# A two-step graph layer: the first step's guess kept as a logarithm, and the packed list's flags made by one comparison

## The chip, the cores and the metric

The kernel runs on one NeuronCore of a Trainium2 chip. A core has five engines that work on their own queues, each in order, [...]: TensorE (PE in the profile; its weight loads are PEld), VectorE (DVE), ScalarE (ACT), GpSimd (POOL) and SyncE (SP, which here only starts DMAs). The metric is the time of one execution on the device in microseconds (us); three runs of the kernel before gave 1349.75, 1350.31 and 1355.44 us, median 1350.31 us.

## The reference, cut to what matters

The input is x (3327 rows of 256) and a sparse matrix adj (3327 x 3327, about four entries in a row beside the diagonal). The rows are normalised and rectified, and a graph layer of two steps runs on the result h:

```python
R = S + eye(N);  R = R / R.sum(-1)            # S is adj
for n in range(2):
    A = top_p_attention(Xa, W1, W2, W3)       # softmax of q k^T, only the largest entries
    Xf = R @ Xf                               # that make up 0.9 of a row's sum
    Xa = A @ Xa
    Z = Z + Xf @ U1[n].T + Xa @ U2[n].T
out = x + layernorm(h + Z) * ln_g + ln_b
```

In each row of the attention the entries are kept from the largest down until their sum reaches 0.9 of the whole. So each row needs a threshold: the value below which the entries sum to at most 0.1 of the row's total Z.

## The kernel before, in words

The 3327 rows are padded to 26 tiles of 128 rows (NP = 3328 columns). For each of the two steps and each tile the kernel makes the 128 x 3328 exponentials `e` of the logits, finds each row's threshold, sets what is below it to zero, turns `e` on TensorE (`Sums.turn`, L809, copied out of PSUM by ScalarE at L811) and multiplies it with the node features (`Sums.sum`, L823).

**The threshold.** It is not searched for by sorting. `guessed` (L616) makes a first guess for each row from Z and from moments of the logits (the columns `ms` that `project` makes on GpSimd at L541 to L545). All the working values are columns of one small tile `g` of 128 x 17, named `col(k)`. In step one, `measured_once` (L635) then sends two passes over the row through ScalarE (L633, once Relu, once Sign) to measure how much lies under the guess, and moves the guess with what they gave; the result is `col(16)`. `settle` (L723) uses it: VectorE keeps what is under the guess in `w` (L729), takes the eight largest of each of 20 segments (L734), the 40 largest of those (L741, L743), finds the exact threshold among them, and masks `e` in place (L763). `prove` checks at the end of each step that every row's threshold is certain; a flag that counts the failing rows decides at the very end whether a second program (`search_graph_layer`) does the whole layer anew by bisection. In step two `measured_twice` takes three passes; the change does not touch it.

**The sparse product.** adj is not multiplied as a whole. `listed` (L836) finds, for each of the 26 rows of tiles, which columns hold an entry: VectorE takes the largest absolute value of each column strip (L853) and `max` gives a list of up to 16 columns per partition. Four of them are fetched directly; those from the fifth on (`DIRECT` to `LIST`) are packed together over the partitions. For that, `over[:, t]` counts how many a partition has beyond four (L865), `packed` (L870) has TensorE sum these counts over the partitions in front (matmul with `upto`, L875; ScalarE copies the sum at L876), and VectorE makes a 128 x 128 matrix `oh` of flags: flag (p, k) is set where place k lies among the places that partition p fills, that is between the sum and the sum plus the count (two comparisons, L879 and L880). `gathered` (L882) uses `oh` in a matmul, picks one column number per partition and writes it as the fifth index (L893, L894). Then GpSimd starts gathers (indirect DMAs): five of columns of adj (`ac`, L900) and five of rows of the features (`xg`, L921) for each tile in step one, and five of `xg` in step two. `diffuse` (L929) multiplies them.

**What sets the order.** The order is written out by hand. Each piece of work is a Python generator, and each `yield` ends one portion of it. `PLAN[step]` holds seven strings (slots k = 0 to 6) for a tile; each letter takes one portion: `m` measured, `d` settle, `c` settle's remainder of the tile before, `w` the exponentials, `q` the next tile's queries, `p` packed, `h` gathered, `a` listed, `g` one gather, `e` first_end, `s` spread, `o` asked_for. In step one:

```python
PLAN = (("gmdsssa", "gmcdsssa", "edawwpg", "gmsdga", "gmspdea", "ohgdawwqg", "gehmgq"), ...
```

So `measured_once` of the tile after the current one takes its portions in slots 0 (guess), 1 (Relu pass), 3 (Sign pass), 4 and 6, and `packed` in slots 2 and 4; ten gathers are spread over the seven slots. Every engine executes its instructions in the order of this text (a dependency between neighbours is added at L1236). Each gather also waits for the last ScalarE instruction that the text has ahead of it (L1209), so that the gathers are spaced out. The tiles `ac` and `xg` have two buffers each, the transposed `eT` three, the PSUM tile `pt` two.

Of the kernel before, what the change touches and what calls it, by code (L numbers as in the profile page):

```python
# [9 lines left out]
F32 = mybir.dt.float32  # L10
# [3 lines left out]
AF = mybir.ActivationFunctionType  # L14
ALU = mybir.AluOpType
# [3 lines left out]
P = 128  # L19
# [4 lines left out]
NP = NT * P  # L24
# [6 lines left out]

SCALE = 1.9
BITS = 27
FIRST = 2.0 ** -7
assert 0.1 * SCALE / N > 2.0 ** -15


# [1 line left out]
def search_graph_layer(  # L39
# [13 lines left out]
    nc = tc.nc  # L53
# [8 lines left out]
    small = ctx.enter_context(tc.tile_pool(name="small", bufs=4))  # L62
# [85 lines left out]
    def nucleus(es, z):  # L148
        n = len(es)
        thr = small.tile([P, 2], F32, tag="thr", name="thr")  # L150
        cand = small.tile([P, 2], F32, tag="cand", name="cand")
        ncand = small.tile([P, 2], F32, tag="ncand", name="ncand")
        over = small.tile([P, 2], F32, tag="over", name="over")
        cnt = small.tile([P, 2], F32, tag="cnt", name="cnt")
        mass = small.tile([P, 2], F32, tag="mass", name="mass")
        low = small.tile([P, 2], I32, tag="low", name="low")
        candi = cand.bitcast(I32)
        nc.vector.tensor_scalar(thr, z, TOP_P, None, ALU.mult)
        nc.vector.memset(cand, FIRST)
        for k in range(BITS - 1, -1, -1):  # L160

            nc.vector.tensor_scalar(ncand, cand, -1.0, None, ALU.mult)
            for a in range(n):
                ja = scan.tile([P, NP], U8, tag="ja", name="ja")
                nc.scalar.activation(ja, es[a], AF.Relu, bias=ncand[:, a : a + 1],
                                     accum_out=over[:, a : a + 1])
                jv = scan.tile([P, NP], U8, tag="jv", name="jv")
                nc.vector.tensor_scalar(jv, es[a], cand[:, a : a + 1], None, ALU.is_ge, ALU.add,
                                        accum_out=cnt[:, a : a + 1])
            nc.vector.tensor_tensor(mass, cand, cnt, ALU.mult)  # L170
            nc.vector.tensor_tensor(mass, mass, over, ALU.add)
            nc.vector.tensor_tensor(low, mass, thr, ALU.is_lt)

            nc.vector.tensor_scalar(low, low, k, (1 << k) >> 1,
                                    ALU.logical_shift_left, ALU.bitwise_or)
            nc.vector.tensor_tensor(candi, candi, low, ALU.bitwise_xor)

        rc = small.tile([P, 2], F32, tag="rc", name="rc")  # L180
        nc.vector.reciprocal(rc, cand)
        nc.vector.tensor_scalar(ncand, cand, -1.0, None, ALU.mult)
        lim = small.tile([P, 2], F32, tag="lim", name="lim")
        for a in range(n):
            c = slice(a, a + 1)
            e = es[a]
            nc.vector.scalar_tensor_tensor(e, e, cand[:, c], e, ALU.is_ge, ALU.mult,
                                           accum_out=mass[:, c])
            eq = scan.tile([P, NP], U8, tag="jv", name="eq")
            nc.vector.tensor_scalar(eq, e, cand[:, c], None, ALU.is_equal)  # L190
            nth = scan.tile([P, NP], I16, tag="nth", name="nth")
            nc.vector.tensor_tensor_scan(nth, eq, eq, 0.0, ALU.add, ALU.max)

            nc.vector.tensor_sub(lim[:, c], thr[:, c], mass[:, c])
            nc.vector.scalar_tensor_tensor(lim[:, c], lim[:, c], rc[:, c], nth[:, NP - 1 : NP],
                                           ALU.mult, ALU.add)
            nc.vector.tensor_scalar(lim[:, c], lim[:, c], 1.0, None, ALU.add)
            nc.vector.scalar_tensor_tensor(eq, nth, lim[:, c], eq, ALU.is_ge, ALU.mult)
            nc.vector.scalar_tensor_tensor(e, eq, ncand[:, c], e, ALU.mult, ALU.add)
# [113 lines left out]
BIG = 1.0e30  # L313
LNBIG = 69.0
# [2 lines left out]
ROUNDS = (5, 6)  # L317
PG = (0.72168716, 3.51308980, -3.48705157)
PK = (3.57528079, -2.54929187, 0.86603878)
OFFSET = (18.0, 14.0)  # L320
TOPK = 8 * max(ROUNDS)
LNY = 0.25 * math.log(0.72)

# [6 lines left out]
FIRST = 8 * P  # L330
# [6 lines left out]
DIRECT = 4  # L337
LIST = 16
# [7 lines left out]
def guess_graph_layer(ctx, tc, x, adj, w1t, w2t, w3t, u1t, u2t, ln_g, ln_b, out, flag):  # L346
    nc = tc.nc
# [14 lines left out]
    V, G, S, PE = nc.vector, nc.gpsimd, nc.scalar, nc.tensor  # L362
# [265 lines left out]
    def con(k):  # L628
        return one[:, k : k + 1]
# [5 lines left out]
    def measured_once(r):  # L635
        e, ms = r["e"], r["ms"]


        col = guessed(r, small.tile([P, 17], F32, tag="g", name="g"))
        S.activation(col(4), col(2), AF.Square, bias=con(4))  # L640
        S.activation(col(11), col(4), AF.Identity, scale=ms(5), bias=ms(6))
        S.activation(col(1), col(0), AF.Exp, scale=-1.0, bias=con(5))
        G.tensor_scalar(col(7), col(9), 0.5, None, ALU.mult)
        G.tensor_scalar(col(8), col(9), 0.5 * NP, None, ALU.mult)
        G.tensor_scalar(col(5), col(1), OFFSET[0], None, ALU.mult)
        G.tensor_scalar(col(10), col(9), col(5), 1.0, ALU.mult, ALU.add)
        yield
        oa = small.tile([P, 3], F32, tag="oa", name="oa")
        through(e, AF.Relu, col(9), -1.0, oa[:, 0:1])
        yield  # L650
        through(e, AF.Sign, col(9), -1.0, oa[:, 1:2])
        yield
        S.activation(col(3), oa[:, 0:1], AF.Identity, scale=-1.0, bias=col(8))
        S.activation(col(4), oa[:, 1:2], AF.Relu, scale=col(7), bias=col(3))
        S.activation(col(6), col(4), AF.Ln, scale=col(1), bias=con(2))
        S.activation(col(3), col(4), AF.Square, scale=col(1), bias=con(1))
        S.activation(col(3), col(3), AF.Ln, scale=0.5, bias=col(10))
        S.activation(col(3), col(3), AF.Identity, scale=-1.0, bias=col(6))
        S.activation(col(3), col(3), AF.Exp, scale=col(11))
        yield  # L660

        V.tensor_scalar(col(5), oa[:, 1:2], NP - 31.0, BIG, ALU.is_gt, ALU.mult)
        V.tensor_scalar(col(6), col(4), col(1), 0.35, ALU.mult, ALU.is_lt)
        V.scalar_tensor_tensor(col(5), col(6), BIG, col(5), ALU.mult, ALU.add)
        V.tensor_scalar(col(3), col(3), 1.0e20, col(9), ALU.min, ALU.mult)
        V.tensor_tensor(col(16), col(3), col(5), ALU.add)

    def measured_twice(r):
        e, ms = r["e"], r["ms"]
# [166 lines left out]
    def listed():  # L836
# [10 lines left out]
        for k, (t, j0, n) in enumerate(pieces):  # L847
            at = ahead
            if k + 1 < len(pieces):
                ahead = asked(*pieces[k + 1])  # L850
            if j0 == 0:
                fm = small.tile([P, NT], F32, tag="fm", name="fm", bufs=2)
            V.tensor_reduce(fm[:, j0 : j0 + n], at[:, :n], AX.X, ALU.max, apply_absolute_value=True)  # L853
            if j0 + n < NT:
                yield
                continue
            V.scalar_tensor_tensor(fm, fm, 0.0, back, ALU.is_gt, ALU.mult)
            V.memset(fm[:, t : t + 1], 0.0)
            ls = lists[:, t, :]
            V.max(ls[:, :8], fm)  # L860
            V.match_replace(fm, ls[:, :8], fm, 0.0)
            V.max(ls[:, 8:LIST], fm)
            G.tensor_scalar(index[:, t, :DIRECT], ls[:, :DIRECT], -1.0, float(NONE), ALU.mult, ALU.add)
            of = small.tile([P, LIST], F32, tag="of", name="of", bufs=2)
            V.tensor_scalar(of[:, DIRECT:], ls[:, DIRECT:LIST], 0.0, None, ALU.is_gt, ALU.add,  # L865
                            accum_out=over[:, t : t + 1])
            done.append(t)
            yield

    def packed(t):  # L870

        assert t in done
        ls, ov = lists[:, t, :], over[:, t : t + 1]
        pb = ps_t.tile([P, 4, P], F32, tag="pt", name="pb")
        PE.matmul(pb[:, 0, :1], upto, ov, start=True, stop=True)  # L875
        S.copy(ls[:, LIST:], pb[:, 0, :1])  # L876
        yield
        ohs[t] = oh = small.tile([P, P], F32, tag="oh", name="oh", bufs=2)
        V.tensor_scalar(oh, place, ov, ls[:, LIST:], ALU.subtract, ALU.is_lt)  # L879
        V.scalar_tensor_tensor(oh, place, ls[:, LIST:], oh, ALU.is_ge, ALU.mult)  # L880

    def gathered(t):  # L882
        oh = ohs.pop(t)
# [7 lines left out]
        yield  # L891
        of = small.tile([P, LIST], F32, tag="of", name="of", bufs=2)
        V.scalar_tensor_tensor(of[:, :n], place[:, :n], nth, lo, ALU.is_equal, ALU.mult, accum_out=nth)  # L893
        G.tensor_scalar(index[:, t, DIRECT:], nth, -1.0, float(NONE), ALU.mult, ALU.add)  # L894

    def adjacent(t):
# [83 lines left out]
        V.tensor_copy(flag, pf[:1, 0, :1])  # L980

    own_of = {}
    live, ohs, acs, xgs, done, early = {}, {}, {}, {}, [], {}
    none = iter(())

    def run(work, n=99):
# [294 lines left out]
```

## Time and profile before

| | us |
|---|---|
| median of three runs | 1350.31 |
| the profiled execution | 1350.64 |
| its span, first to last instruction | 1348.9 |
| TensorE matmul busy | 1268.1 |
| VectorE busy | 1186.8 |
| ScalarE busy | 1081.0 |
| GpSimd busy | 997.2 |
| mean granted TensorE clock | 0.982 |

Step one's tiles run from about 100 to 745 us, the turn to step two until about 850 us, step two's tiles to the end. A busy time is the time in which an engine had an instruction in work. Matmuls are pipelined and their ends are modelled, so their busy times overlap, and spans on GpSimd are rough. A row of the timeline gives the start in us, the length in us, the engine, the line, the operation and its operands, and in brackets how long the engine had been idle and what ended the wait ("issue": nothing that the profile shows).

### The profile page before, as it was taken

What the parts mean: (1) busy time and instruction counts of PE and PEld (TensorE: products, weight loads), DVE (VectorE), ACT (ScalarE), POOL (GpSimd) and SP (SyncE); (2) the same over time, 40 slices, a digit from 0 to 9 for tenths busy, and PEclk for the clock granted to TensorE, in tenths of its full rate; (3) what the DMA queues carried; (4) which work ended last, traced back from release to release, by engine and by line L of the source; (5) the groups of instructions that cost most, each with busy time, mean ns of one, the idle gap of its engine ahead of it and who ended that gap; (6) DMA issues with size and microseconds to landing.
All of it is one profiled execution on the core that took longest, in us unless ns stands there. A gap on an engine that the chain in (4) does not pass through costs nothing.

```text
span 1348.9 us, 22270 instructions
## 1 busy us (share of the span) xinstructions
PE 1268.1 (94%) x6495; PEld 976.0 (72%) x6495; DVE 1186.8 (88%) x3637; ACT 1081.0 (80%) x2368; POOL 997.2 (74%) x1399
## 2 busy tenths in 40 slices
PE   5989899999999999999999579999999999999985
PEld 4635687877778777787877457777777777777774
DVE  6877899999999999999990689899998999999993
ACT  5475788798888879888863789899998999999841
POOL 5114788888878878887873578888888888888832
PEclk9999999999999999999999779999999999999998
DMA  8644545455454544445332212221212222122200
GB/s 277 221 157 141 160 136 144 134 144 147 133 153 133 140 138 142 144 135 152 106 104 86 75 55 60 78 89 54 91 59 85 62 82 90 52 91 64 81 21 24
DMA packets 92645, 149.79 MB, mean 111 GB/s; under 512 B 15425, under 2 KB 59072, under 8 KB 92512
## 3 DMA queue, kind: packets, MB, share of 16 engines
q1 hardware_dynamic: 75056, 105.37, 24.6%
q0 software_dynamic: 16640, 42.69, 12.1%
q8 instruction: 54, 0.88, 0.3%
q14 instruction: 79, 0.65, 0.2%
q10 hardware_dynamic: 816, 0.20, 0.1%
HBM read 120.93 MB, written 27.28 MB: 110 GB/s over the span
## 4 chain that ended last, share of the span: by engine, by line
PE 51%; DVE 20%; ACT 12%; POOL 11%; issue 3%; DMA 2%; SPq 0%; POOLq 0%; DVEq 0%; ACTq 0%
PE pa L823 22%; ACT ja L633 7%; PE pl L600 7%; PE pt L809 6%; PE pr L929 5%; POOL xg L921 5%; DVE w L729 4%; PE pz L942 3%; DVE cand L734 3%; DVE e L763 3%; PE pz L1011 2%; POOL g L676 2%; DVE bb L741 1%; DVE cand L743 1%; ACT e L604 1%
## 5 line engine op out<-in xcount | busy, mean ns | idle before, releaser
L823 PE MATMUL pa<-xw,eT 128*128 128x256 f32 x1352 | 323.6, 384 | 3.6 <-DVE s L953 3.6
L633 ACT ACTIVATE ja<-e,g 128x3328 uint8<-128x3328 f32 x106 | 325.7, 3072 | 0.1
L823 PE MATMUL pa<-x,eT 128*128 128x256 f32 x1352 | 323.1, 380 | 0.0
L823 PEld LDWEIGHTS pa<-xw,eT 128*128 128x128 f32 x1352 | 250.7, 190 | 52.5 <-issue 14.4
L823 PEld LDWEIGHTS pa<-x,eT 128*128 128x128 f32 x1352 | 243.7, 191 | 25.8
L734 DVE MAX8 cand<-w 128x8 f32<-128x168 f32 (+1 forms) x1040 | 253.7, 319 | 0.0
L811 ACT COPY eT<-pt 128x512 f32<-128x512 f32 (+1 forms) x364 | 199.5, 555 | 48.8 <-PE pt L809 47.7
L921 POOL DMA_INDIRECT xg<-bx,index x130 | 188.7, 1451 | 54.7 <-issue 24.4
L900 POOL DMA_INDIRECT ac<-in_adj,index x130 | 162.9, 1253 | 63.8 <-issue 28.2
L809 PE MATMUL pt<-ident,e 128*128 128x128 f32 x1144 | 176.6, 277 | 17.3 <-DVE e L760 9.4
L809 PEld LDWEIGHTS pt<-ident,e 128*128 128x128 f32 x1144 | 139.8, 144 | 60.5 <-issue 36.0
L921 POOL DMA_INDIRECT xg<-vx,index x130 | 152.5, 1173 | 34.3 <-issue 30.3
L729 DVE SCALAR_TENSOR_TENSOR w<-e,g 128x3328 f32<-128x3328 f32 x44 | 162.7, 3698 | 3.1 <-ACT g L714 3.0
L929 PE MATMUL pr<-xg,ac 128*128 128x257 f32 (+1 forms) x520 | 141.0, 395 | 8.4 <-DVE s L1119 6.8
L763 DVE SCALAR_TENSOR_TENSOR e<-e,rec 128x3328 f32<-128x3328 f32 x40 | 148.3, 3707 | 0.6
L604 ACT ACTIVATE e<-pl 128x832 f32<-128x832 f32 x132 | 112.9, 859 | 27.3 <-PE pl L600 21.9
L929 PEld LDWEIGHTS pr<-xg,ac 128*128 128x128 f32 x520 | 93.9, 194 | 34.0 <-issue 14.1
L600 PE MATMUL pl<-both,qT 64*128 64x416 f32 x416 | 93.0, 546 | 9.3 <-ACT e L604 7.0
L741 DVE MAX8 bb<-cand 128x8 f32<-128x160 f32 x286 | 92.7, 324 | 6.4
L853 DVE TENSOR_REDUCE fm<-at 128x4 f32<-128x512 f32 (+1 forms) x133 | 84.7, 637 | 13.3 <-DMA at<-in_adj 13.3
L600 PE MATMUL pl<-after,qT 64*128 64x416 f32 x416 | 95.4, 552 | 0.5 <-ACT e L604 0.5
L633 ACT ACTIVATE ja<-x,g 128x3328 uint8<-128x3328 f32 x24 | 73.7, 3070 | 0.0
(260 smaller groups left out, 2129.8 us busy)
## 6 DMA issues: line engine op xcount, KB each, us to landing
at<-in_adj SPq DMA_DIRECT2D x114, 256.0 KB
cx<-ac SPq DMA_DIRECT2D x26, 384.0 KB
ac<-cx SPq DMA_DIRECT2D x26, 384.0 KB
wide<-in_adj SPq DMA_DIRECT2D x8, 832.0 KB
e<-in_adj SPq DMA_DIRECT2D x6, 832.0 KB
own<-bx SPq DMA_DIRECT2D x26, 128.5 KB
x<-in_x SPq DMA_DIRECT2D x13, 256.0 KB
xr<-in_x SPq DMA_DIRECT2D x26, 128.0 KB
```

Of the source, the lines that this page charges most:

```text
L600: PE.matmul(pl[:, a, :wd], qT[p, :], keys_of(step, a).rearrange("p a b -> p (a b)")[:, c : c + wd], start=True, stop=True)
L604: S.activation(e.rearrange("p (a n) -> p a n", a=2)[:, :, c : c + wd], pl[:, :, :wd], AF.Exp, accum_out=za[:, n : n + 1])
L633: S.activation(ja, e, f, bias=guess, scale=sign, accum_out=total)
L729: V.scalar_tensor_tensor(w, e, col(16), e, ALU.is_lt, ALU.mult, accum_out=d2)
L734: V.max(cand[:, 8 * s : 8 * s + 8], w[:, s * SEG : min(NP, (s + 1) * SEG)])
L763: V.scalar_tensor_tensor(e, e, at(1), e, ALU.is_ge, ALU.mult, accum_out=ra)
L809: PE.transpose(pt[:, j, :], e[:, (j0 + j) * P : (j0 + j + 1) * P], ident)
L811: S.copy(eT[:, :w, :], pt[:, :w, :])
L823: PE.matmul(self.pa, eT[:, c - 4 * k, :], self.xa[:, j, :], start=c == 0, stop=c == NT - 1)
L900: G.indirect_dma_start(out=ac[:, k, :], out_offset=None, in_=rows, in_offset=bass.IndirectOffsetOnAxis(ap=index[:, t, k : k + 1], axis=0), ...
L921: G.indirect_dma_start(out=xg[:, k, :w], out_offset=None, in_=rows, in_offset=bass.IndirectOffsetOnAxis(ap=index[:, t, k : k + 1], axis=0))
L929: PE.matmul(pr[:, :w], ac[:, k, :], own if k == KT - 1 else xg[:, k, :w], start=k == 0, stop=k == KT - 1)
```

## The change

Four edits, all in step one's small work:

- The guess is kept as a logarithm. Before, ScalarE made ln of the measured share and ln of a denominator, took the difference, and the exponential of it times `col(11)`; VectorE then put a guard of 1e30 on rows of two kinds, capped the factor, multiplied by the first guess `col(9)` and added the guard (five VectorE instructions on 128 x 1). Now the exponent is put together on GpSimd, with the logarithm of the first guess (`col(12)`) and the guard (LNBIG = 69) added to it and a cap at 80, and a single ScalarE Exp in slot 6 gives `col(16)`. The denominator loses its squared term, and its constant goes from 18 to 19. `col(11)` moves from ScalarE to GpSimd.
- The columns beyond four are counted by ScalarE (a Sign pass over 12 entries with a sum) in place of VectorE, in `counted`, which is called when `gathered` of two tiles earlier ends, or by `packed` if that has not happened.
- The flags `oh` come from one comparison: GpSimd makes half a count and a squared half count in the small tile `nh`, ScalarE makes the middle of the filled places and the 128 x 128 squares of the distances to it, and VectorE compares these with the squared half count.
- A constant of the second program is renamed, because its name was used twice.

```diff
-FIRST = 2.0 ** -7
+LOWEST = 2.0 ** -7
...
-        nc.vector.memset(cand, FIRST)
+        nc.vector.memset(cand, LOWEST)
...
 ROUNDS = (5, 6)
 PG = (0.72168716, 3.51308980, -3.48705157)
 PK = (3.57528079, -2.54929187, 0.86603878)
-OFFSET = (18.0, 14.0)
+OFFSET = (19.0, 14.0)
 TOPK = 8 * max(ROUNDS)
 LNY = 0.25 * math.log(0.72)
...
         col = guessed(r, small.tile([P, 17], F32, tag="g", name="g"))
         S.activation(col(4), col(2), AF.Square, bias=con(4))
-        S.activation(col(11), col(4), AF.Identity, scale=ms(5), bias=ms(6))
         S.activation(col(1), col(0), AF.Exp, scale=-1.0, bias=con(5))
         G.tensor_scalar(col(7), col(9), 0.5, None, ALU.mult)
         G.tensor_scalar(col(8), col(9), 0.5 * NP, None, ALU.mult)
+        G.tensor_scalar(col(11), col(4), ms(5), ms(6), ALU.mult, ALU.add)
         G.tensor_scalar(col(5), col(1), OFFSET[0], None, ALU.mult)
         G.tensor_scalar(col(10), col(9), col(5), 1.0, ALU.mult, ALU.add)
+        G.tensor_scalar(col(12), col(3), ms(3), ms(8), ALU.mult, ALU.add)
         yield
         oa = small.tile([P, 3], F32, tag="oa", name="oa")
         through(e, AF.Relu, col(9), -1.0, oa[:, 0:1])
         yield
         through(e, AF.Sign, col(9), -1.0, oa[:, 1:2])
         yield
+        G.tensor_scalar(col(5), oa[:, 1:2], NP - 31.0, BIG, ALU.is_gt, ALU.mult)
+        G.tensor_scalar(col(5), r["Z"], 0.035, col(5), ALU.mult, ALU.add)
         S.activation(col(3), oa[:, 0:1], AF.Identity, scale=-1.0, bias=col(8))
         S.activation(col(4), oa[:, 1:2], AF.Relu, scale=col(7), bias=col(3))
         S.activation(col(6), col(4), AF.Ln, scale=col(1), bias=con(2))
-        S.activation(col(3), col(4), AF.Square, scale=col(1), bias=con(1))
-        S.activation(col(3), col(3), AF.Ln, scale=0.5, bias=col(10))
-        S.activation(col(3), col(3), AF.Identity, scale=-1.0, bias=col(6))
-        S.activation(col(3), col(3), AF.Exp, scale=col(11))
-        yield
-        V.tensor_scalar(col(5), oa[:, 1:2], NP - 31.0, BIG, ALU.is_gt, ALU.mult)
-        V.tensor_scalar(col(6), col(4), col(1), 0.35, ALU.mult, ALU.is_lt)
-        V.scalar_tensor_tensor(col(5), col(6), BIG, col(5), ALU.mult, ALU.add)
-        V.tensor_scalar(col(3), col(3), 1.0e20, col(9), ALU.min, ALU.mult)
-        V.tensor_tensor(col(16), col(3), col(5), ALU.add)
+        S.activation(col(10), col(10), AF.Ln)
+        G.tensor_scalar(col(14), col(4), col(5), LNBIG, ALU.is_lt, ALU.mult)
+        G.tensor_tensor(col(12), col(12), col(14), ALU.add)
+        G.tensor_scalar(col(6), col(6), col(10), col(11), ALU.subtract, ALU.mult)
+        G.tensor_scalar(col(6), col(6), col(12), 80.0, ALU.add, ALU.min)
+        yield
+        S.activation(col(16), col(6), AF.Exp)
     def measured_twice(r):
         e, ms = r["e"], r["ms"]
...
             V.match_replace(fm, ls[:, :8], fm, 0.0)
             V.max(ls[:, 8:LIST], fm)
             G.tensor_scalar(index[:, t, :DIRECT], ls[:, :DIRECT], -1.0, float(NONE), ALU.mult, ALU.add)
-            of = small.tile([P, LIST], F32, tag="of", name="of", bufs=2)
-            V.tensor_scalar(of[:, DIRECT:], ls[:, DIRECT:LIST], 0.0, None, ALU.is_gt, ALU.add,
-                            accum_out=over[:, t : t + 1])
             done.append(t)
             yield
+    def counted(t):
+        if t not in done or t in counts:
+            return
+        counts.append(t)
+        of = small.tile([P, LIST], F32, tag="of", name="of", bufs=2)
+        S.activation(of[:, DIRECT:], lists[:, t, DIRECT:LIST], AF.Sign, accum_out=over[:, t : t + 1])
     def packed(t):
-        assert t in done
+        counted(t)
+        assert t in counts
         ls, ov = lists[:, t, :], over[:, t : t + 1]
+        nh = small.tile([P, 3], F32, tag="nh", name="nh", bufs=2)
+        G.tensor_scalar(nh[:, 0:1], ov, -0.5, 0.5, ALU.mult, ALU.add)
+        G.tensor_scalar(nh[:, 1:2], ov, ov, 0.25, ALU.mult, ALU.mult)
         pb = ps_t.tile([P, 4, P], F32, tag="pt", name="pb")
         PE.matmul(pb[:, 0, :1], upto, ov, start=True, stop=True)
         S.copy(ls[:, LIST:], pb[:, 0, :1])
-        yield
+        S.activation(nh[:, 2:3], pb[:, 0, :1], AF.Identity, scale=-1.0, bias=nh[:, 0:1])
         ohs[t] = oh = small.tile([P, P], F32, tag="oh", name="oh", bufs=2)
-        V.tensor_scalar(oh, place, ov, ls[:, LIST:], ALU.subtract, ALU.is_lt)
-        V.scalar_tensor_tensor(oh, place, ls[:, LIST:], oh, ALU.is_ge, ALU.mult)
+        S.activation(oh, place, AF.Square, bias=nh[:, 2:3])
+        yield
+        V.tensor_scalar(oh, oh, nh[:, 1:2], None, ALU.is_lt)
     def gathered(t):
         oh = ohs.pop(t)
...
         yield
         of = small.tile([P, LIST], F32, tag="of", name="of", bufs=2)
         V.scalar_tensor_tensor(of[:, :n], place[:, :n], nth, lo, ALU.is_equal, ALU.mult, accum_out=nth)
+        if valid(t + 2):
+            counted(t + 2)
         G.tensor_scalar(index[:, t, DIRECT:], nth, -1.0, float(NONE), ALU.mult, ALU.add)
     def adjacent(t):
...
         V.tensor_copy(flag, pf[:1, 0, :1])
     own_of = {}
-    live, ohs, acs, xgs, done, early = {}, {}, {}, {}, [], {}
+    live, ohs, acs, xgs, done, counts, early = {}, {}, {}, {}, [], [], {}
     none = iter(())
     def run(work, n=99):
```

More of the change, by code (lines that the diff above doesn't have):

```diff
@@ L876, in packed @@
         S.copy(ls[:, LIST:], pb[:, 0, :1])
+        S.activation(nh[:, 2:3], pb[:, 0, :1], AF.Identity, scale=-1.0, bias=nh[:, 0:1])
+        ohs[t] = oh = small.tile([P, P], F32, tag="oh", name="oh", bufs=2)
+        S.activation(oh, place, AF.Square, bias=nh[:, 2:3])
         yield
-        ohs[t] = oh = small.tile([P, P], F32, tag="oh", name="oh", bufs=2)
-        V.tensor_scalar(oh, place, ov, ls[:, LIST:], ALU.subtract, ALU.is_lt)
-        V.scalar_tensor_tensor(oh, place, ls[:, LIST:], oh, ALU.is_ge, ALU.mult)
+        V.tensor_scalar(oh, oh, nh[:, 1:2], None, ALU.is_lt)
     def gathered(t):
```

## The prediction

> **What bounds the kernel now.** I read the page's shares first, then a table of stages, then the chain of waits inside the steady part of step one, and last the timelines of GpSimd, VectorE and ScalarE over one tile there.
>
> ```profile
> span 1348.9 us, 22270 instructions
> ...
> PE 1268.1 (94%) x6495; PEld 976.0 (72%) x6495; DVE 1186.8 (88%) x3637; ACT 1081.0 (80%) x2368; POOL 997.2 (74%) x1399
> ```
>
> The shares put POOL last, but they mix two steps. The stages 138 to 375 us and 375 to 702 us are the steady part of step one, the only step that the change edits (columns: stage, length, then busy time of PE, PEld, DVE, ACT, POOL, clock, DMA share, GB/s):
>
> ```profile
> 138.00:375.00 237.00, 232.41 (x1234) 184.50 (x1234) 227.76 (x701) 196.54 (x484) 201.01 (x235) 0.99 0.49 141
> 375.00:702.00 327.00, 327.00 (x1746) 259.72 (x1746) 312.28 (x969) 272.22 (x675) 266.03 (x310) 1.00 0.47 135
> ```
>
> PE is full (98 and 100%), DVE 96 and 95%, ACT 83%, POOL 85 and 81%. The chain of waits from 200 to 700 us is TensorE alone, with no step on another engine:
>
> ```profile
> by line: PE pa L823 47.4%; PE pl L600 13.3%; PE pt L809 12.9%; PE pr L929 11.5%; PE pz L942 7.2%; PE pk L485 1.9%; PE pb L875 1.3%; PE pt L474 0.9%; PE pq L523 0.9%; PE pk L488 0.9%; PE pq L525 0.9%; PE pg L499 0.6%; PE po L886 0.5%
> ```
>
> So VectorE at 95% costs nothing here: TensorE has no gap to give back, and the change leaves its queue as it is. What matters is who is next to full. POOL's timeline of a tile answers that:
>
> ```profile
> 402.61 3.61 POOL L946 TENSOR_TENSOR sv<-sv,x 128x256 f32<-128x256 f32 x1 [0.38 <-issue]
> 406.37 0.97 POOL L921 DMA_INDIRECT xg<-bx,index  x1 [0.15 <-ACT mq L532]
> 407.64 3.87 POOL L921 DMA_INDIRECT xg<-bx,index  x1 [0.30 <-issue]
> 411.81 0.95 POOL L921 DMA_INDIRECT xg<-bx,index  x1 [0.30 <-ACT g L622]
> ...
> 418.28 0.26 POOL L643 TENSOR_SCALAR g<-g 128x1 f32<-128x1 f32 x1
> 418.60 0.21 POOL L644 TENSOR_SCALAR g<-g 128x1 f32<-128x1 f32 x1
> ...
> 419.87 1.03 POOL L921 DMA_INDIRECT xg<-bx,index  x1 [0.41 <-ACT lists L876]
> ```
>
> ```profile
> 401.96 3.68 DVE L763 SCALAR_TENSOR_TENSOR e<-e,rec 128x3328 f32<-128x3328 f32 x1
> ...
> 407.01 3.68 DVE L729 SCALAR_TENSOR_TENSOR w<-e,g 128x3328 f32<-128x3328 f32 x1
> ```
>
> Each gather is 0.95 us and 0.30 ahead of it, ten times a tile. Two instructions a tile last 2.9 to 3.3 us longer than their like, each just while VectorE makes one of its two 3.68 us passes. From 138 to 375 us the gaps between POOL's instructions are the usual ones only (0.30 ahead of a gather, about 0.1 elsewhere); afterwards some are longer. Summed over 138 to 702 us, what exceeds the usual is 12.5 us, the largest 2.99 at 636.14 and 2.00 at 379.17. That is POOL's whole slack: 0.5 us per tile of 23.85 us (L541 starts at 201.55 and, 19 tiles later, at 654.74). A busy 81% is a nearly full queue.
>
> **What the Trainium skill says.** "SBUF — State Buffer", section "Who interferes with whom", says that a VectorE instruction with two SBUF inputs and a GpSimd one that reads SBUF exclude each other and "the other **fully blocks**"; the rows above agree (0.95 becomes 3.87, 0.74 becomes 3.61), so a busy POOL loses nearly two whole passes a tile. "Perfetto Trace Analysis", section "GPSIMD Engine Instruction", says to price GpSimd work by the spacing of starts; I do. The same page, section "Optimizing Scalar/DVE Operations", warns that moving work between VectorE and GpSimd may not help, since they share a port.
>
> **The change, part by part, per tile.** PE and SP keep the same instructions in the same order; no DMA is added or moved.
>
> VectorE loses L662 to L666 (406.18 to 406.87: 0.69 us), L865 (0.17) and one of L879 and L880 (398.48 to 399.12 together; 0.3 saved): about 1.2 us. Worth nothing while TensorE is full.
>
> ScalarE loses L641, L656 to L659 (0.387 + 0.372 + 0.294 + 0.295 + 0.294 = 1.64 us) and gains an Ln (0.29), an Exp (0.29), an Identity out of PSUM (0.27 as L890), a 128x128 Square (0.26 as the copy L528) and a Sign with a sum (0.37 as L610): 1.48 us. Nothing.
>
> POOL gains ten instructions on 128x1. Spacings: L643 to L644 0.32, L644 to L645 0.29, L697 to L698 0.37, L708 to L709 0.40, L710 to L711 0.18, L711 to L712 0.38, L676 to L677 0.41 (the free one at 752.76). So two with pairs of `ms` columns 2 x 0.41, two `nh` 2 x 0.30, two on col(5) 2 x 0.37, col(14) 0.40, the add 0.20, two on col(6) 2 x 0.38: 3.52 us. Bounds: 2.7 if all cost 0.27, 4.1 if all cost 0.41. Below nothing is excluded, as POOL loses no instruction.
>
> L643, once a tile, starts 26 times, three of them before 138 us, where POOL idles anyway (waits of 13.9 us for a DMA and 15.7 for ScalarE). That leaves 23 tiles: 23 x 3.52 = 81.0 us; less the 12.5 us of slack: 68.5 us by which POOL's queue no longer fits. Ends: 23 x 2.7 - 12.5 = 50 and 23 x 4.1 - 12.5 = 82.
>
> Is the lateness passed on? Gathers alone have room: xg goes out at 335 to 350 us and TensorE uses it at 363 to 367, so TensorE could wait through some 10 us once. But the change adds waits without room. `packed` now has ScalarE's Identity wait for nh[0], which POOL runs behind the gather at 419.87; today's copy stands here:
>
> ```profile
> 419.66 0.16 ACT L876 COPY lists<-pb 128x1 f32<-128x1 f32 x1
> ```
>
> nh[0] would be done near 421.3, 1.6 us later, or 2.4 with the two new instructions at the guess. Behind the Identity on ScalarE stand the Square, the eT copies that empty TensorE's two transpose buffers, and the Sign pass of 3.07 us; VectorE's `is_lt` waits for Square and nh[1]. ScalarE's last Exp waits for col(6), and VectorE's pass L729 for the Exp. So POOL's lateness reaches TensorE each tile, and step one runs at POOL's pace, about 23.85 + 3.52 - 0.54 = 26.8 us. After 702 us POOL has idle stretches again (10.2 and 7.9 us), and step two's code is unchanged: both only shift. Start-up: the first two guesses trade 1.3 us of other engines for 1.7 on POOL: under 1 us.
>
> The sum is made against the profiled execution, 1350.64 us (0.3 above the median of 1350.31): 1350.6 + 68.5 = **1419 us**. Its own range is 1390 to 1442: the ends of the price, less 10 for the one-off room below, and 10 above for stalls, since back-to-back short instructions can lose up to 7.4 us a tile to the two passes where dense tiles lose 5.8 to 6.6.
>
> **Rivals.** *POOL and ScalarE take turns waiting.* col(14) on POOL needs col(4) from ScalarE. From the copy at 419.66 to L654's end at 424.46 is 4.8 us, with Identity and Square 5.4; POOL from nh[0] to col(14) needs 0.3 + 4 x 1.25 + 0.74 = 6.0. The margin is 0.6 us; if ScalarE is 2 us late there, POOL idles about 1.5 us: 23 x 1.5 = 35, so 1454. For it: ScalarE already waits for TensorE in the tile (1.52 us at 408.14). Against: POOL's own stalls widen the margin.
>
> *The new work fits.* If the stalls shrink by what is added (VectorE's passes falling on moments where POOL waits), TensorE stays full: 1350, within 0.5%. Against: from 138 to 375 us POOL has no such moment.
>
> *VectorE sets the pace after all* (other side). At 95%, if its lateness were what delays TensorE, 1.2 us x 26 = 31 us would go: 1319. It decides if TensorE's time in steady tiles contains waits for VectorE; the table of waits has one of 2.9 us from 138 to 375 us and the chain none after 200.
>
> *The change doesn't do what it says*: should the coarser logarithmic guess miss in one row, the search runs too: 27 rounds x 52 tiles x a 3.07 us ScalarE pass is over 4300 us more. The guards are the same two, so 2%.
>
> **How the numbers follow.** Chances: POOL-paced near 1419: 0.66; with ScalarE's turns 0.21; fits 0.06; VectorE 0.05; search 0.02. The range of 8 in 10 is 1388 to 1456: the first case's range and most of the second, leaving about 0.17 out. 0.5% (6.8 us) is about what a measurement of this kernel tells from no change. Faster 0.05, same 0.06, slower 0.89.
>
> **What would show it.** Right: in 138 to 760 us PE's busy share falls to about 89%, POOL's gaps are the usual only, L541's spacing is about 26.8 us, ScalarE has waits for POOL `nh` and col(6), and step two keeps its length. L541 at 24 us with a full PE shows the sum wrong; a spacing over 28 with POOL waiting for ScalarE before col(14) shows the first rival.

## The result, and the profile after

The changed kernel takes 1455.21 us (median of four runs, 1454.39 to 1456.18) where the kernel before takes 1350.18: 1.0761 times as long, 95% interval 1.0731 to 1.0792. It is slower by 105 us. The forecast's direction and its range (1388 to 1456) hold, the latter barely; the time named, 1419, is 36 us too low.

The page's first lines after:

```profile
span 1454.0 us, 22382 instructions
...
PE 1300.4 (89%) x6495; PEld 993.8 (68%) x6495; DVE 1155.9 (79%) x3429; ACT 1070.4 (74%) x2394; POOL 1073.1 (74%) x1659
```

VectorE is busy for 31 us less, ScalarE for 11 us less, POOL for 76 us more, and POOL's share is 74% as before: the share names nobody. The same two stages as before (length, then busy time of PE, PEld, DVE, ACT, POOL, clock, DMA share, GB/s):

```profile
138.00:375.00 237.00, 208.09 (x1049) 160.25 (x1049) 180.36 (x520) 163.51 (x428) 189.48 (x280) 0.96 0.43 123
375.00:702.00 327.00, 289.57 (x1474) 226.63 (x1473) 253.17 (x742) 230.40 (x585) 264.96 (x389) 0.95 0.42 118
```

TensorE, full before, is at 88 and 89%. TensorE, VectorE and ScalarE all do fewer instructions in the same stretch (1049 matmuls for 1234, 1474 for 1746); POOL alone does more, in no more busy time (189.48 us for 201.01, 264.96 for 266.03). The granted clock of TensorE is lower (0.96 and 0.95 for 0.99 and 1.00), but it does not make the loss: the run with the guess alone, below, loses 58 us at 0.98 and 1.00 in these two stages. And the chain that ended last, by engine, is spread over four engines (first line before, second after):

```profile
PE 51%; DVE 20%; ACT 12%; POOL 11%; issue 3%; DMA 2%; SPq 0%; POOLq 0%; DVEq 0%; ACTq 0%
...
PE 31%; DVE 29%; ACT 15%; POOL 14%; issue 7%; DMA 2%; SPq 0%; POOLq 0%; DVEq 0%; ACTq 0%
```

POOL's timeline in the changed kernel: `nh` and two gathers in one tile, then the last gathers of that group and the guess's exponent in the tile before it:

```profile
445.68 0.19 POOL L880 TENSOR_SCALAR nh<-over 128x1 f32<-128x1 f32 x1
445.84 0.26 POOL L881 TENSOR_SCALAR nh<-over 128x1 f32<-128x1 f32 x1
446.87 1.00 POOL L911 DMA_INDIRECT ac<-in_adj,index  x1 [0.76 <-ACT oh L887]
448.18 0.95 POOL L911 DMA_INDIRECT ac<-in_adj,index  x1 [0.30 <-issue]
```

```profile
421.67 4.22 POOL L911 DMA_INDIRECT ac<-in_adj,index  x1 [1.26 <-ACT ja L633]
426.20 0.96 POOL L911 DMA_INDIRECT ac<-in_adj,index  x1 [0.30 <-issue]
427.22 0.25 POOL L654 TENSOR_SCALAR g<-oa 128x1 f32<-128x1 f32 x1
427.58 0.27 POOL L655 TENSOR_SCALAR g<-rec,g 128x1 f32<-128x1 f32 x1
427.96 0.29 POOL L660 TENSOR_SCALAR g<-g 128x1 f32<-128x1 f32 x1
428.34 0.19 POOL L661 TENSOR_TENSOR g<-g 128x1 f32<-128x1 f32 x1
428.52 0.38 POOL L662 TENSOR_SCALAR g<-g 128x1 f32<-128x1 f32 x1
428.99 0.31 POOL L663 TENSOR_SCALAR g<-g 128x1 f32<-128x1 f32 x1
429.27 0.72 POOL L957 TENSOR_TENSOR sv<-sv,x 128x256 f32<-128x256 f32 x1
```

Between gathers 0.30 us is usual. Two of a tile's ten gathers now wait longer, on average 0.77 us behind ScalarE's Square (L887) and 1.28 behind its Sign pass (L633). Less the usual 0.30 each, that is 1.45 us per tile in which POOL, the engine that is late, does nothing. Ahead of L660, where col(14) needs ScalarE's col(4), there is no such gap. ScalarE at the same place:

```profile
439.56 0.16 ACT L884 COPY lists<-pb 128x1 f32<-128x1 f32 x1
445.90 0.26 ACT L885 ACTIVATE nh<-pb,nh 128x1 f32<-128x1 f32 x1 [6.18 <-POOL nh L880]
446.19 0.40 ACT L887 ACTIVATE oh<-place,nh 128x128 f32<-128x128 f32 x1
```

It stands 6.18 us until POOL reaches `nh`, and only then makes the Square and the Sign pass for which POOL's gathers have to wait. So in each tile ScalarE waits for POOL, and then POOL waits for ScalarE. The table of waits from 200 to 780 us (engine, line, what it waited for: sum, times, longest):

```profile
ACT nh L885 <- POOL nh L880: 84.6, 20, 8.0
PEld pt L808 <- ACT nh L885: 72.1, 20, 7.4
...
DVE w L728 <- ACT g L665: 41.7, 18, 2.9
...
POOL ac L911 <- ACT ja L633: 26.8, 21, 1.3
...
POOL ac L911 <- ACT oh L887: 15.4, 20, 0.8
```

TensorE's idle time is behind the same Identity (72.1 us of weight loads that wait). Before, POOL's gathers waited for the Sign pass six times in the same window:

```profile
POOL ac L900 <- ACT ja L633: 3.2, 6, 1.2
```

**Where the 105 us are.** I split the time between two starts of L541 on POOL (once a tile) into the usual length of each instruction (the lower quartile of its line), what it lasted beyond that, and the gaps. Before, over 18 tiles: 23.70 = 13.90 + 5.77 + 4.03 us. After, over 17 tiles: 28.01 = 16.72 + 6.11 + 5.18. So a tile costs 4.31 more: 2.82 of instructions, 0.34 of stalls, 1.15 of gaps (the two gathers' 1.45, some new spacing, less the 0.5 of slack that was there). 23 tiles x 4.31 = 99 us. The second tile's pass of VectorE (L729 before, L728 after) starts at 113.99 instead of 110.25, 3.7 more. From the first such pass of step two to the end it is 580.5 us before (to 1348.9) and 581.3 after (to 1454.0): step two is only moved. The two passes, before and after:

```profile
768.44 3.68 DVE L729 SCALAR_TENSOR_TENSOR w<-e,g 128x3328 f32<-128x3328 f32 x1 [1.97 <-ACT g L714]
...
872.68 3.68 DVE L728 SCALAR_TENSOR_TENSOR w<-e,g 128x3328 f32<-128x3328 f32 x1 [1.98 <-ACT g L713]
```

### The profile page after: what moved, and what is told of

It is laid out like the page before. It is cut to its first block, busy times and chain, and to the rows that moved or that the text cites. A ratio compares the mean times of both kernels' runs of the same rounds, so it can differ in the third digit from the quotient of the medians.

```text
span 1454.0 us, 22382 instructions
## 1 busy us (share of the span) xinstructions
PE 1300.4 (89%) x6495; PEld 993.8 (68%) x6495; DVE 1155.9 (79%) x3429; ACT 1070.4 (74%) x2394; POOL 1073.1 (74%) x1659
## 4 chain that ended last, share of the span: by engine, by line
PE 31%; DVE 29%; ACT 15%; POOL 14%; issue 7%; DMA 2%; SPq 0%; POOLq 0%; DVEq 0%; ACTq 0%
PE pa L822 13%; DVE w L728 7%; ACT ja L633 7%; DVE cand L733 5%; POOL xg L932 4%; PE pt L808 4%; PE pl L600 4%; DVE e L762 3%; PE pz L953 3%; POOL ac L911 2%; PE pr L940 2%; DVE x L762 2%; ACT e L604 2%; DVE bb L740 2%; DVE cand L742 1%
## 5 line engine op out<-in xcount | busy, mean ns | idle before, releaser
L822 PE MATMUL pa<-x,eT 128*128 128x256 f32 x1352 | 339.4, 395 | 0.0
L633 ACT ACTIVATE ja<-e,g 128x3328 uint8<-128x3328 f32 x106 | 325.1, 3067 | 0.1
L822 PEld LDWEIGHTS pa<-x,eT 128*128 128x128 f32 x1352 | 253.8, 199 | 29.5
L808 PE MATMUL pt<-ident,e 128*128 128x128 f32 x1144 | 181.3, 282 | 90.5 <-ACT nh L885 71.7
L911 POOL DMA_INDIRECT ac<-in_adj,index x130 | 189.1, 1455 | 82.3 <-ACT ja L633 29.4
L932 POOL DMA_INDIRECT xg<-bx,index x130 | 184.4, 1418 | 46.3 <-issue 24.6
L728 DVE SCALAR_TENSOR_TENSOR w<-e,g 128x3328 f32<-128x3328 f32 x44 | 163.1, 3706 | 58.8 <-ACT g L665 45.0
L932 POOL DMA_INDIRECT xg<-vx,index x130 | 133.6, 1028 | 34.0 <-issue 30.2
L600 PE MATMUL pl<-both,qT 64*128 64x416 f32 x416 | 92.4, 543 | 9.4 <-DVE e L1028 4.7
L600 PE MATMUL pl<-after,qT 64*128 64x416 f32 x416 | 95.0, 550 | 0.7 <-ACT e L604 0.7
L885 ACT ACTIVATE nh<-pb,nh 128x1 f32<-128x1 f32 x26 | 6.8, 262 | 95.3 <-POOL nh L880 95.3
```

What stands on the lines that cost most here:

```text
L600: PE.matmul(pl[:, a, :wd], qT[p, :], keys_of(step, a).rearrange("p a b -> p (a b)")[:, c : c + wd], start=True, stop=True)
L633: S.activation(ja, e, f, bias=guess, scale=sign, accum_out=total)
L728: V.scalar_tensor_tensor(w, e, col(16), e, ALU.is_lt, ALU.mult, accum_out=d2)
L808: PE.transpose(pt[:, j, :], e[:, (j0 + j) * P : (j0 + j + 1) * P], ident)
L822: PE.matmul(self.pa, eT[:, c - 4 * k, :], self.xa[:, j, :], start=c == 0, stop=c == NT - 1)
L911: G.indirect_dma_start(out=ac[:, k, :], out_offset=None, in_=rows, in_offset=bass.IndirectOffsetOnAxis(ap=index[:, t, k : k + 1], axis=0), ...
```

## The experiments

Two theories stood against each other. A: POOL's queue has become longer than a tile, whoever waits for it. B: the new waits between ScalarE and POOL cost the time, not the length. Each run was timed beside the kernel before; I give the ratio to it with its 95% interval, and the difference in us as the ratio's excess times 1350.

**Ten instructions that nobody reads.** Constants in, a scratch tile out, at the places of the change's ten (two at the guess, two in `packed`, six after the Sign pass):

```diff
+    def idle_work(kinds):
+        dz = small.tile([P, 8], F32, tag="dz", name="dz")
+        z = lambda k: dz[:, k : k + 1]
+        for n, kind in enumerate(kinds):
+            x = z(n - 1) if n else of_s[:, 3:4]
+            if kind == "t":
+                G.tensor_tensor(z(n), x, half[:, 1:2], ALU.add)
+            elif kind == "i":
+                G.tensor_scalar(z(n), x, -0.5, 0.5, ALU.mult, ALU.add)
+            elif kind == "p":
+                G.tensor_scalar(z(n), x, half[:, 1:2], 0.25, ALU.mult, ALU.mult)
+            else:
+                G.tensor_scalar(z(n), x, half[:, 1:2], half[:, 2:3], ALU.mult, ALU.add)
...
+        idle_work("dd")
...
+        idle_work("iiptdp")
...
+        idle_work("ip")
```

> The kernel before with ten instructions on 128x1 added to GpSimd's queue per tile of step one, of the kinds and at the places of the change's ten, reading constants and read by nobody; nothing else is changed, so no engine waits for them. Theory A (the length of GpSimd's queue sets the pace): 23 tiles x 3.5 us less 12.5 us of slack, about +68, so 1419 us (1400 to 1432), L541's spacing near 26.8 us. Theory B (the new waits between ScalarE and GpSimd do it, not the length): within 10 us of 1350.

Measured: 1422.75 us, 1.0532 (1.0486 to 1.0578), +72 us. TensorE's share falls although no dependency was added (the stage 375 to 702 us, columns as above):

```profile
375.00:702.00 327.00, 304.99 (x1560) 235.07 (x1560) 277.29 (x874) 248.38 (x618) 271.69 (x407) 0.97 0.44 126
```

The lateness goes out through waits that were always there. Two stand out from 200 to 750 us. VectorE waits for a strip of adj (`at`). In all 19 cases SyncE has issued that DMA just behind the store of `sv`, for which it waits until POOL has made `sv` (third line, SyncE's own waits; before, that line has 124.6 us, and VectorE waits 1.8 us in all for such strips). ScalarE waits for col(8), which POOL makes at the guess:

```profile
DVE fm L869 <- DMA at<-in_adj: 65.3, 19, 6.1
ACT g L669 <- POOL g L658: 48.5, 20, 4.7
...
SPq L965 <- POOL sv L963: 239.5, 18, 17.1
```

Which of the two holds TensorE up is not shown.

VectorE's passes are 26.74 us apart (mean of 18; 23.67 before). The length alone costs 72 of the 105 us. A holds for that part; that length costs nothing, as B has it, falls. What is left, some 31 us, is not in this run.

**Three such instructions**, all after the Sign pass (`idle_work("iid")`):

> As the run with ten, with three such instructions per tile, all after the Sign pass (about 1.05 us). A: the slack of 12.5 us takes half of 23 x 1.0, so about +11, 1361 us (1352 to 1368). B: 1350.

Measured: 1367.56 us, 1.0112 (1.0075 to 1.0149), +15 us (10 to 20). Within this interval the slack is as small as the gaps had shown; three instructions on single columns, about 1 us a tile, are enough to be seen.

**The guess alone.** `measured_once` and OFFSET of the change; `listed`, `packed` and `gathered` as before.

> The kernel before with the logarithmic guess alone: eight more GpSimd instructions per tile (2.9 us), ScalarE's last Exp waits for GpSimd, the counting and the flags as before. A: 23 x 2.9 - 12.5 = +54, so 1405 us (1390 to 1420). B, if the Identity's wait for nh is what counts: 1350 to 1360; if the Exp's wait counts, anything up to 1450.

Measured: 1409.66 us, 1.0428 (1.0391 to 1.0466), +58 us, as A said (+54). The lateness reaches VectorE through the Exp, in two steps (waits from 200 to 750 us):

```profile
ACT g L665 <- POOL g L663: 85.6, 20, 6.4
DVE w L728 <- ACT g L665: 73.1, 21, 5.5
```

These are long, and the time is still about what A gives for the eight instructions: a wait for the late engine costs little or nothing of its own here.

**The counting and the flags alone.** `counted`, `packed` and `gathered` of the change; the guess as before.

> The kernel before with the counting on ScalarE and the flags from one comparison alone: two more GpSimd instructions per tile (0.6 us), and ScalarE's Identity waits for one of them. A: 23 x 0.6 is about the slack, so 1350 to 1357 us. B: the Identity's wait and the two gathers that wait for ScalarE's Square and Sign passes behind it (1.45 us of idle GpSimd per tile in the changed kernel) come back, about +35, so 1385 us.

Measured: 1377.61 us, 1.0198 (1.0160 to 1.0236), +27 us, for two instructions of 0.19 and 0.26 us. That is three quarters of B's +35, and A had foreseen 7 us at most: most of it is no queue length, and B's mechanism is here. POOL's waits from 138 to 702 us show it (0.3 of each is the usual gap):

```profile
POOL ac L912 <- ACT ja L633: 28.2, 22, 1.3
...
POOL ac L912 <- ACT oh L888: 17.1, 22, 1.0
```

22 x 1.45 = 32, plus about 0.4 us a tile for the two instructions, less the 12.5 us of slack: 29 us.

**All ten placed elsewhere.** `col(11)`, `col(12)` and both `nh` on ScalarE, the six of the exponent on VectorE ahead of the Exp:

```diff
-        G.tensor_scalar(nh[:, 0:1], ov, -0.5, 0.5, ALU.mult, ALU.add)
-        G.tensor_scalar(nh[:, 1:2], ov, ov, 0.25, ALU.mult, ALU.mult)
+        S.activation(nh[:, 0:1], ov, AF.Identity, scale=-0.5, bias=half[:, 1:2])
+        S.activation(nh[:, 1:2], ov, AF.Square, scale=0.5)
...
-        G.tensor_scalar(col(11), col(4), ms(5), ms(6), ALU.mult, ALU.add)
+        S.activation(col(11), col(4), AF.Identity, scale=ms(5), bias=ms(6))
+        S.activation(col(12), col(3), AF.Identity, scale=ms(3), bias=ms(8))
...
-        G.tensor_scalar(col(12), col(3), ms(3), ms(8), ALU.mult, ALU.add)
...
         yield
+        V.tensor_scalar(col(5), oa[:, 1:2], NP - 31.0, BIG, ALU.is_gt, ALU.mult)
+        V.tensor_scalar(col(5), r["Z"], 0.035, col(5), ALU.mult, ALU.add)
+        V.tensor_scalar(col(14), col(4), col(5), LNBIG, ALU.is_lt, ALU.mult)
+        V.tensor_tensor(col(12), col(12), col(14), ALU.add)
+        V.tensor_scalar(col(6), col(6), col(10), col(11), ALU.subtract, ALU.mult)
+        V.tensor_scalar(col(6), col(6), col(12), 80.0, ALU.add, ALU.min)
         S.activation(col(16), col(6), AF.Exp)
```

> The whole change with its ten GpSimd instructions put elsewhere: col(11), col(12) and both nh on ScalarE, the guard and the exponent (six instructions) on VectorE in slot 6, ahead of ScalarE's Exp; GpSimd's queue is as before. If GpSimd's queue and the waits for it are the whole cause: 1345 to 1358 us. If the other edits (the Exp in front of VectorE's pass, the Square in front of the flags) cost something too: 1360 to 1400.

Measured: 1358.91 us, 1.0047 (1.0032 to 1.0062), +6 us, just outside the first expectation. TensorE is full again:

```profile
375.00:702.00 327.00, 326.04 (x1737) 258.09 (x1738) 308.40 (x935) 276.79 (x745) 271.66 (x313) 1.00 0.47 135
```

VectorE's passes are 23.87 us apart (23.67 before), and the second tile's pass starts at 115.79 us, 5.5 later than before; most of the 6 us lies ahead of it. There TensorE's weight loads for the logits (L600) wait 3.7 us for a copy on VectorE (L1028), which they do not before; why VectorE is later there stays open. In steady tiles the new formulas cost next to nothing; where their instructions stand costs 7%.

**Only `nh` on ScalarE**, the eight of the guess left on POOL (the first four lines of that diff):

> The whole change with both nh made by ScalarE; GpSimd keeps eight of the ten. Queue length and hand-over both count (A and B together): the queue's part of the guess alone stays, the hand-over at the flags goes, so about 1409 us as the guess alone (1400 to 1420). A alone: 1455 less 23 x 0.6, 1441. B alone: 1350 to 1360.

Measured: 1412.95 us, 1.0435 (1.0398 to 1.0473), +59 us, the guess alone's +58. The two `nh` on POOL and the waits that they bring are worth 44 us.

**`nh` earlier.** The same ten on POOL, but the two `nh` at the end of slot 6 of the tile before, ahead of the `ms` columns and three gathers:

```diff
         G.tensor_scalar(index[:, t, DIRECT:], nth, -1.0, float(NONE), ALU.mult, ALU.add)
+        if t + 2 in counts:
+            halves(t + 2)
```

where `halves` makes the two, once per tile, and `packed` takes them from it.

> The whole change with GpSimd's two nh instructions moved from slot 2 to the end of slot 6 of the tile before, right after the fifth index, so that ScalarE's Identity finds them done; the queue is as long as in the change. A and B together: the hand-over's part of 33 us goes, 1422 us as with ten idle instructions (1412 to 1432). A alone: 1455. B alone: 1350 to 1360.

Measured: 1427.17 us, 1.0541 (1.0506 to 1.0577), +73 us. The hand-over is gone, the length is left. ScalarE's waits from 200 to 750 us still sum to over 100 us, now for the Exp's input and for col(8):

```profile
ACT g L665 <- POOL g L663: 91.5, 21, 6.7
...
ACT g L656 <- POOL g L647: 26.2, 20, 2.0
```

**Without the gathers' extra wait.** The change, with the dependency of each gather on the last ScalarE instruction ahead of it (L1209 before) left out; it carries no data.

> The whole change without the extra wait of each gather for the last ScalarE instruction ahead of it (no data depends on it). If the hand-over costs through the two gathers that wait behind ScalarE's Square (0.77 us) and Sign pass (1.29 us) while ScalarE had waited for nh: 23 x 1.45 = 33 us go, 1422 us (1412 to 1435). If it costs through ScalarE's own wait alone: 1450 to 1457.

Measured: 1425.65 us, 1.0536 (1.0498 to 1.0573), +72 us. ScalarE still waits for `nh` (from 200 to 750 us):

```profile
ACT nh L885 <- POOL nh L880: 63.7, 20, 5.1
```

and 30 us are gone. So what ScalarE waits is not the cost; POOL's idle time behind it is.

**The kernel before without that wait**, the control:

> The kernel before without the gathers' extra wait for ScalarE: a control for the run of the change without it. TensorE is full there and GpSimd waits 12.5 us in all, so 1350 us (1342 to 1356). If the wait itself costs time by its own, up to 30 us less.

Measured: 1350.46 us, 0.9981 (0.9961 to 1.0001). Nothing by itself: POOL was not behind enough for it to matter.

**Both remedies**, `nh` early and no extra wait:

> The change with both remedies, nh early and the gathers' extra wait gone. If both take away the same hand-over, nothing is added: 1420 to 1428 us, the queue's length alone. If each takes away a part of its own: 1395 us or so.

Measured: 1425.57 us, 1.0525 (1.0486 to 1.0565), +71 us. They take away the same 30 us.

**The counting and the flags with `nh` on ScalarE**, the guess as before:

> The counting and the flags' part alone, with both nh made by ScalarE, so that GpSimd has no new instruction and ScalarE waits for none of its own: 1345 to 1355 us if the part's 26 us are the hand-over and two queue places; 1360 or more if the Square and the Sign on ScalarE cost something.

Measured: 1351.85 us, 0.9987 (0.9974 to 1.0001): no difference from the kernel before that can be told. TensorE is full, and VectorE's relief, small in this run (535 us busy for 540 in the two stages), brings nothing that can be told, as foreseen:

```profile
375.00:702.00 327.00, 327.00 (x1746) 259.19 (x1745) 310.83 (x930) 285.33 (x756) 273.15 (x310) 1.00 0.47 135
```

No version tried is faster than the kernel before by more than its measurement tells.

## Why the prediction was right, and where it was not

*The bound.* TensorE was full and VectorE's 95% cost nothing: right as far as it was tried. The two kernels that keep POOL's queue as it was (all ten elsewhere, and the flags with `nh` on ScalarE) gain nothing. They relieve VectorE by only 11 and 5 us of 540 in the two stages, so the whole relief of 31 us was not tried; that it would gain nothing rests on TensorE having no gap before.

*The slack.* 12.5 us, read from the gaps: borne out as far as the runs tell. Three instructions already cost 15 us, where 11 were expected.

*The price of the ten.* Forecast 3.52 us a tile. In the tile shown above the six after the Sign pass take 2.05 us from start to start (427.22 to 429.27), the two `nh` 0.42 with the gap ahead of the gather taken off, and the two at the guess only 0.52, because the gap ahead of the next gather shrinks from 0.41 to 0.15. Together 2.99: the forecast was too high by 0.5, against which stalls rose by 0.34 a tile. The net, +72 us for ten idle instructions, is close to the forecast's +68.5. That part of the sum stands, helped by two errors that in part cancel.

*How the lateness is passed on.* Right in kind: ScalarE waits for `nh` and VectorE's pass for the Exp. Foreseen was that this makes POOL's pace everybody's, at no further price.

*What failed: that POOL, once late, waits for nothing.* The sum had no term for the gathers' waits on ScalarE, since before they cost nothing. With ScalarE stopped at the Identity until POOL passes, the Square and the Sign pass come late, and two gathers per tile wait for them: 23 x 1.45 = 33 us, and 28 to 30 us by the runs (1455.2 less 1427.2 and 1425.7). The first rival had this size (1454) and the kind (POOL and ScalarE in turns), but named the wrong place: it let POOL wait at col(14), where the trace has no gap. That its number is 1 us from the measured one is luck, and so is that the range held: the main case's own range ended at 1442, and it was this rival that stretched the whole to 1456. The dependency was described ahead of the prediction and left out of the rival. It should have been asked of each POOL instruction behind the new wait which ScalarE instruction it needs.

*Start-up.* Under 1 us was forecast; the second tile's pass starts 3.7 us later. Ahead of it TensorE's weight loads for the logits wait 3.9 us for VectorE's copy L1028, as in the run with all ten elsewhere.

*The other rivals.* The new work did not fit, VectorE did not set the pace, the search did not run.

## What to carry to other kernels

An engine at 81% busy can be full: add the usual gap ahead of each of its DMAs and the stalls that it can't avoid, and see what idle time is left over per tile; three instructions on single columns were too many here. Moving work off an engine that is busy but waited for by nobody bought nothing here, and the queue that took it paid. A wait of an on-time engine for the late one cost nothing by itself that these runs could tell; what cost time was the wait of the late engine behind it, so follow each new wait one step further, through every old dependency that leads back.

## What was not expected of the hardware

On ScalarE an instruction on 128x1 took 0.19 to 0.20 us with plain numbers as scale and bias (Ln L659, Exp L665), 0.29 with one column of scalars (L622 to L624) and 0.39 with two (L657, L658); 0.29 had been assumed for the Ln and the Exp. The 128x128 Square out of SBUF with a column as bias took 0.40, against 0.26 assumed from the plain copy L528 out of PSUM.
